# A two-layer image model on one core: the last image's row and column terms through a constant selection tile, and the spectral taps loaded earlier

## The chip, the cores and the metric

The kernel runs on one core of one Trainium2 chip. The metric is the time of one execution on the device in microseconds (us). Three runs of the kernel before gave 9375.59, 9384.07 and 9384.95, so the median is 9384.07 us. Everything is float32.

The profile speaks of five engines: PE (TensorE, matrix multiplies; its weight loads are listed apart as PEld), DVE (VectorE), ACT (ScalarE), POOL (GpSimd) and SP (SyncE, which here does nothing but issue DMA transfers, in the order of its queue). A fp32 matrix multiply shows as two or more PE instructions, a transpose as one. PEclk is the TensorE clock that was granted, 1.00 being full speed.

## The reference

The input `x` is four images of 64 x 64 tokens with 128 channels. Two layers follow, each with a convolution-like part and a feed-forward part; all normalizations (`ln`) are per token over the 128 channels.

```python
# layer 0
x = x + ss2d(ln(x))                 # four selective scans per image, 256 channels, 16 states
t = x as [B, 4096, 128]
p = softmax(ln(t) @ gate_w.T + gate_b, over the 4096 tokens)   # 64 experts
v, idx = top_k(p per expert, 8)                  # each expert picks 8 tokens
pooled = sum_k v[k] * ln(t)[idx[k]]              # [64 experts, 128]
o = gelu(pooled @ w1 + b1) @ w2 + b2             # 128 -> 512 -> 128, per expert
t[idx[k]] += v[k] * o                            # scattered back
# layer 1, on the image as [row m, column k, channel]
n = ln(x)
x = x + n @ Wself.T + (sum_k n) @ Wm.T + (sum_m n) @ Wk.T
t = x as tokens; u = ln(t)
t = t + stu(u)        # one of four segment lengths per a one-hot weight
```

Here `(sum_k n) @ Wm.T` is one 128-vector per row of the image, shared by its 64 columns (the row term), and `(sum_m n) @ Wk.T` is one per column, shared by its 64 rows (the column term). `stu` is the sum of a spectral part (a causal convolution over 4096 tokens with 16 long filters, each followed by a 128 x 128 matrix) and an autoregressive part (`ar`: the token and the two before it, times three 128 x 128 matrices).

## The kernel before, in words

The kernel works through the images in sequence. For each image, sixteen-state scans run in chunks; that is the bulk of the span (`hh`, `db`, `da`, `y` in the profile's groups), and while one image is scanned, the earlier image's experts and layer one (`layer1`), and the front of the next one, are worked off in pieces beside it (`beside`). The last image has nothing to run beside, so what follows its scans is a tail of its own:

- `after_scans` makes the last image's gate logits, transposed: `pT`, 64 experts by 4096 tokens, in a pool named `last`.
- `last_experts` (from L1542). `match_replace` makes `rest`, the probabilities with the top eight of each expert struck out (L1617), and the difference `pT - rest` leaves only the picked ones in `pT`. In `turn_back` (L1632) 64 x 128 blocks of `pT` are turned to token-major by matrix multiplies with `turned`, a diagonal matrix of `1/ssum` (one over the softmax sum per expert), eight blocks to a bank `pk_ps`. `pool` (L1640) then gathers: 32 multiplies accumulate into `po_ps`. Then come 64 weight-streamed expert multiplies (`h1_ps`, `h2_ps`, shown as `h_ps`; L1665, L1697), with `w_t` tiles in a ring of 26 buffers refilled by SP; the bias (L1678), the gelu, the transposes, and at last `outE`, the 64 x 128 outputs of the experts, times `1/ssum`.
- `last_layer1` (from L1728). It has two phases, each a loop `for k in range(10)` over eight groups of 512 tokens (eight image rows), staggered so that group `k` is begun while `k-1` and `k-2` are finished. **Phase one**, per group: four multiplies `sc_ps` of `pT` blocks by `outE` (the scatter, L1786), added to `x2` (L1813); normalization; four transposes `xn_ps` (L1773); `sum_blocks` (`rs_ps`, L1367), four multiplies with a constant that yield the 64 column sums and the 8 row sums of the group, copied to `rs_l`; then the bank `z_ps`: per 128-token block (two image rows) one multiply by `wself_t` (L1792) and two 64-row ones, `row_total` broadcast over 64 columns by `wm_t` (L1801), accumulated in the same bank. `add_total` sums the column totals over the groups on GpSimd into `mk`. VectorE adds `z_ps` to `x2` (L1821). Between the phases one multiply by `wk_t` (L1825) makes the column terms, `cols`, a 128 x 128 tile that is the same for every 128-token block. **Phase two**, per group: `cols` added to `x2` (L1851), normalization, store to `u_d` (L1849), transposes `u_ps`, ScalarE's copy `uT_l`, twelve multiplies `ar_ps` (L1839), the weighted add (L1860) and the store to `x3_d` (L1863).
- `spectrum` (from L1893). It opens with the loads of `taps` (four DMAs, 128 x 4096, L1903) and of the first two `vt` tiles (four each, L1923), then issues the loads `zs` of the normalized tokens (`u_d`, L2041). `taps_of` multiplies `vt` with `taps` into `sp_ps` (L1914), evicted to `wt` (L1918); between its steps the last image's tokens are transformed (`slots_of`). The rest of the spectrum's blocks follow, then `endings`.

What sets the order: the program is written once and a scheduler in the framework orders each engine's instructions by dependence and readiness, with tile pools limiting how many buffers are alive. A tile that is taken from a pool waits for the buffers that held its place before; a pool that opens where another closed waits for the latter's readers. Inside `last_layer1`, `pin(begin)` fixes the order of TensorE, ScalarE, VectorE and GpSimd as written. SP's queue of DMA issues is not pinned. `bank` takes the next of eight one-bank PSUM tiles. `kr` is the pool `last` (right side of the on-chip memory), which is closed before `spectrum` opens its own pools `sp_t` and `sp_w` on the same side.

Of the kernel before, what the change touches and what calls it, by code (L numbers as in the profile page):

```python
# [110 lines left out]
def kernel(  # L111
# [1433 lines left out]
    def last_experts(b, last, pieces):  # L1545
# [5 lines left out]
        with tc.tile_pool(name="tl", bufs=1) as tl:  # L1551
# [62 lines left out]
            turned = tl.tile([E, E], F32, name="turned_a")  # L1614
            with tc.tile_pool(name="tr", bufs=2) as tr:
# [4 lines left out]
                nc.vector.tensor_scalar(turned, ident[0:E, 0:E], ssum, None, ALU.mult)  # L1620
# [7 lines left out]
                def turn_back(g):  # L1628
                    ps = bank([P, 8, E], "pk_ps")
                    for q in range(8):  # L1630
                        t0 = (8 * g + q) * P
                        nc.tensor.matmul(  # L1632
                            ps[:, q, :], pT[:, t0 : t0 + P], turned, start=True, stop=True
                        )
# [39 lines left out]
            with tc.tile_pool(name="tm", bufs=1) as tm:  # L1674
# [3 lines left out]
                nc.vector.tensor_add(h1, hps, b1t)  # L1678
# [46 lines left out]
        last_layer1(b, pT, outE, x2)  # L1725
        xr.__exit__(None, None, None)

    def last_layer1(b, pT, outE, x2):  # L1728

        with tc.tile_pool(name="ll", bufs=2) as lp:  # L1730
            rs = lp.tile([P, 8, W + 8], F32, name="rs_l", bufs=1)
            mk = lp.tile([P, 2, W], F32, name="mk_l", bufs=1)
            begin = len(traced)
# [41 lines left out]
            for k in range(10):  # L1775
                g = k - 2
                if g >= 0:
# [3 lines left out]
                    add_total(mk, rs, g)  # L1781
                if k < 8:
# [6 lines left out]
                if g >= 0:  # L1789
                    z = ps[g, "z"] = four("z_ps")  # L1790
                    for q in range(4):
# [4 lines left out]
                            start=(q == 0),  # L1796
                            stop=False,
                            skip_group_check=True,
                        )
                        for i in range(2):  # L1800
                            nc.tensor.matmul(  # L1801
                                z[i * W : (i + 1) * W, q, :],
                                row_total(rs, 8 * g + 2 * q + i),
                                wm_t,
                                start=False,
                                stop=(q == 3),
                                skip_group_check=True,
                            )
# [739 lines left out]
```

## Time and profile before

| quantity | value |
|---|---|
| median of 3 runs | 9384.07 us (9375.59 to 9384.95) |
| the profiled execution's own time | 9385.75 us |
| its span | 9383.6 us, 139970 instructions |
| its mean granted TensorE clock | 0.839 |
| PE / DVE / ACT / POOL busy | 78% / 87% / 65% / 68% |

By stages (us from the start of the span; busy time in us):

| stretch | what runs | PE | DVE | ACT | POOL | clock | DMA share |
|---|---|---|---|---|---|---|---|
| 0 to 7650 | fronts, scans, earlier images | 5794.58 | 7337.50 | 5260.52 | 6313.30 | 0.82 | 0.64 |
| 7650 to 7706 | last image: softmax, match | 23.11 | 9.58 | 26.62 | 12.38 | 0.67 | 0.92 |
| 7706 to 7735 | `turn_back`, `pool` | 28.49 | 6.66 | 2.45 | 3.00 | 0.50 | 0.06 |
| 7735 to 7798 | expert multiplies | 57.64 | 2.60 | 3.03 | 1.80 | 0.93 | 0.95 |
| 7798 to 7880 | layer one, phase one | 78.54 | 25.58 | 22.79 | 2.49 | 0.52 | 0.00 |
| 7880 to 7921 | layer one, phase two | 30.79 | 26.29 | 21.79 | 1.29 | 0.87 | 0.33 |
| 7921 to 7935 | spectral loads | 0.00 | 0.44 | 0.00 | 0.00 | 0.63 | 0.99 |
| 7935 to 7986 | first `taps_of`, last image's tokens | 44.56 | 24.01 | 22.09 | 0.00 | 0.80 | 0.65 |
| 7986 to 9200 | spectrum | 1157.72 | 720.83 | 692.97 | 0.00 | 1.00 | 0.34 |
| 9200 to 9384 | last backward block, endings | 114.95 | 47.91 | 23.28 | 0.00 | 0.83 | 0.79 |

How to read it: busy times of different engines overlap, so a row does not add up to its stretch. Where one engine's busy time fills the stretch, that engine sets the pace. Where none does, the chain of waits tells which wait ended last. The granted clock is a mean over the stretch.

### The profile page before, as it was taken

How to read it: one execution, taken by the hardware profiler on the slowest of the kernel's cores; microseconds unless marked ns; L12 is line 12 of the kernel's file. 1: busy time of each engine (PE TensorE's matmuls, PEld its weight loads, DVE VectorE, ACT ScalarE, POOL GpSimd, SP SyncE). 2: the span in 40 equal slices, each digit the busy share in tenths (PEclk: the TensorE clock that was granted, in tenths of full speed). 3: DMA queues.
4: the chain of work that ended last, by engine and by line, in shares of the span. 5: the costliest groups of instructions: out<-in, count | busy, mean ns of one | idle time of the engine just before them, and what ended most of it. 6: DMA issues, size and time to landing. Idle time of an engine off the chain costs nothing.

```text
span 9383.6 us, 139970 instructions
## 1 busy us (share of the span) xinstructions
PE 7330.4 (78%) x45310; PEld 4733.8 (50%) x45310; DVE 8201.4 (87%) x9342; ACT 6075.5 (65%) x11458; POOL 6334.3 (68%) x5822
## 2 busy tenths in 40 slices
PE   7778787677777777697768777867777668999997
PEld 4445454355444555454544554543555445556663
DVE  8999999989999999999999999999999963566663
ACT  6676777657755576776865676875586752555552
POOL 6778788969888788877978798977888850000000
PEclk8888797668778888798878887878887877999998
DMA  5656657658566656657757657847757764333336
GB/s 168 214 192 209 208 191 246 204 181 251 184 206 224 215 173 207 199 187 244 248 179 246 211 184 226 252 167 237 243 174 216 212 208 142 95 95 95 95 94 182
DMA packets 918577, 1806.24 MB, mean 192 GB/s; under 512 B 86592, under 2 KB 476512, under 8 KB 914136
## 3 DMA queue, kind: packets, MB, share of 16 engines
q1 hardware_dynamic: 917848, 1797.30, 59.8%
q8 instruction: 363, 5.95, 0.3%
q14 instruction: 366, 3.00, 0.1%
HBM read 1554.75 MB, written 242.22 MB: 192 GB/s over the span
## 4 chain that ended last, share of the span: by engine, by line
POOL 33%; PE 23%; issue 15%; DVE 11%; DMA 9%; ACT 8%; SPq 1%; POOLq 0%; DVEq 0%; ACTq 0%
POOL hh L2407 25%; PE sp_ps L1914 10%; DVE hh L2394 5%; PE y L2434 4%; DVE wt L1918 3%; DMA bc<-bc_d 2%; DVE db L2388 2%; ACT da L2334 2%; PE dl_ps L2254 2%; POOL hst L2406 2%; POOL dx L2257 1%; POOL ex L2248 1%; DMA yk<-y_d 1%; PE dt_ps L2229 1%; ACT no_sq L362 1%
## 5 line engine op out<-in xcount | busy, mean ns | idle before, releaser
L2407 POOL TENSOR_TENSOR hh<-hh,bc 128x1024 f32<-128x1024 f32 x2048 | 4829.5, 2359 | 331.0 <-DVE hh L2394 179.1
L2394 DVE TENSOR_TENSOR_SCAN hh<-da,hst,db 128x512 f32<-128x512 f32 x3584 | 4387.0, 1266 | 115.0 <-PE y L2434 64.3
L2434 PE MATMUL y<-ident,hh 128*128 128x128 f32 x16384 | 2622.9, 314 | 1100.1 <-POOL hh L2407 1007.2
L2334 ACT ACTIVATE da<-dl,aneg 128x512 f32<-128x512 f32 x4096 | 2775.7, 717 | 1066.9 <-DVE hh L2394 1053.4
L2434 PEld LDWEIGHTS y<-ident,hh 128*128 128x128 f32 x16384 | 2194.5, 162 | 1986.5 <-POOL hh L2407 1339.2
L2388 DVE TENSOR_TENSOR db<-du,bc 128x512 f32<-128x512 f32 x4096 | 2619.8, 684 | 154.5 <-ACT du L2314 111.6
L2406 POOL COPY hst<-hh 128x2 f32<-128x2 f32 x1792 | 336.5, 188 | 699.8 <-DVE hh L2394 618.0
L1918 DVE COPY wt<-sp_ps 128x1024 f32<-128x1024 f32 x512 | 607.3, 1221 | 183.4 <-PE sp_ps L1914 161.5
L1914 PE MATMUL sp_ps<-vt,taps 32*128 32x256 f32 x8192 | 593.2, 401 | 67.4 <-DVE wt L1918 32.6
L2394 DVE TENSOR_TENSOR_SCAN hh<-da,db 128x512 f32<-128x512 f32 x512 | 595.9, 1203 | 19.9 <-ACT no_r L366 9.6
L1918 ACT COPY wt<-sp_ps 128x1024 f32<-128x1024 f32 x512 | 514.9, 1015 | 136.8 <-PE sp_ps L1914 118.4
L1914 PEld LDWEIGHTS sp_ps<-vt,taps 32*128 32x128 f32 x8192 | 396.3, 186 | 260.2 <-DVE wt L1918 190.3
L1918 DVE COPY zs<-sp_ps 128x1024 f32<-128x1024 f32 x132 | 161.7, 1225 | 363.8 <-DMA gq<-dft_out 132.7
L1914 PE MATMUL sp_ps<-wt,ut 128*32 128x256 f32 x8192 | 450.3, 380 | 2.0 <-ACT ut L1918 2.0
L740 PE MATMUL cv_ps<-xh,diag 128*128 128x512 f32 x864 | 398.6, 597 | 4.6 <-ACT sg_v L409 3.2
L2254 PE MATMUL dl_ps<-ex,ident 128*128 128x512 f32 x508 | 308.9, 697 | 116.5 <-POOL ex L2248 111.4
L2229 PE MATMUL dt_ps<-dts,dtw 8*128 8x512 f32 x508 | 350.8, 796 | 56.6 <-ACT sg_v L409 25.9
L2257 POOL TENSOR_TENSOR dx<-dl,xc 128x1024 f32<-128x1024 f32 x127 | 300.2, 2364 | 98.0 <-ACT dl L2255 91.3
L1914 PEld LDWEIGHTS sp_ps<-wt,ut 128*32 128x32 f32 x8192 | 264.0, 110 | 196.7 <-issue 25.3
L2255 ACT COPY dl<-dl_ps 128x512 f32<-128x512 f32 x254 | 147.0, 579 | 330.0 <-PE dl_ps L2254 328.9
L1918 ACT COPY zs<-sp_ps 128x1024 f32<-128x1024 f32 x132 | 133.6, 1012 | 330.0 <-DMA zf<-zs 212.9
L2248 POOL TENSOR_TENSOR ex<-ex,dx 128x1024 f32<-128x1024 f32 x127 | 299.9, 2361 | 49.3 <-ACT dx L2245 38.4
(391 smaller groups left out, 9127.5 us busy)
## 6 DMA issues: line engine op xcount, KB each, us to landing
bc<-bc_d SPq DMA_DIRECT2D x2048, 512.0 KB
xc<-xc_d SPq DMA_DIRECT2D x128, 512.0 KB
y_d<-ys SPq DMA_DIRECT2D x128, 512.0 KB
w1t<-in_w_dram SPq DMA_DIRECT2D x96, 512.0 KB
w2t<-in_w_dram SPq DMA_DIRECT2D x192, 256.0 KB
yk<-y_d SPq DMA_DIRECT2D x128, 256.0 KB
yk<-y_d SPq DMA_DIRECT2D x256, 128.0 KB
zf<-zs SPq DMA_DIRECT2D x512, 64.0 KB
```

What stands on the lines that cost most here:

```text
L740: nc.tensor.matmul(ps, diag[:, h, t, :], xh[:, 8 * g + dy : 8 * g + dy + 8, dx : dx + W], start=(t == 0), stop=(t == 8),)
L1914: tc.keep_in_program_order(nc.tensor.matmul(*args, **kw))
L1918: tc.keep_in_program_order(copy(dst, src))
L2229: nc.tensor.matmul(ps, dtw[:, k, h * P : (h + 1) * P], dts, start=True, stop=True)
L2254: nc.tensor.matmul(ps, ident, t[:, h], start=t is dl, stop=t is w)
L2257: nc.gpsimd.tensor_mul(dx, dl, xc)
L2334: i_act = nc.scalar.activation(das[t][:, h, :], sizes[t // N][0][:, h, :], AF.Exp, scale=aneg[:, tk, h, t % N : t % N + 1],)
L2388: nc.vector.tensor_mul(db[h], dus[i][h], bcs[s][:, 0, :])
L2394: i_dve = nc.vector.tensor_tensor_scan(o, d0, d1, init, ALU.mult, ALU.add)
L2406: nc.gpsimd.tensor_copy(hsts[t // N][:, :, t % N], hhs[t][:, :, last])
L2407: i_pool = nc.gpsimd.tensor_mul(hhs[t], hhs[t], bcs.pop(t)[:, 1:2, :].to_broadcast([P, 2, SC]))
L2434: i_pe = nc.tensor.matmul(ys[c][:, q, h, :], hhs[t][:, h, q * P : (q + 1) * P], ident, is_transpose=True, start=(n == 0 and k > 0 and q % ...
```

## The change

It has four parts.

1. `turn_back` uses plain transposes; `turned` is gone. The factor `1/ssum` is applied later, to the first expert layer's sum: a constant `rows` (built on GpSimd) spreads `ssum` over the 128 partitions of `h1_ps` by one multiply, and the bias add becomes `h * by_row + b1`.
2. In phase one the `wm_t` multiplies are gone from `z_ps`; the row sums of each group are copied on GpSimd into `rt_l`. After the loop, one bank gets the column terms in partitions 0 to 63 (`mk` by `wk_t`) and the row terms in 64 to 127 (`rt_l` by `wm_t`), which ScalarE copies to `both_l`.
3. A constant tile `place_l`, 128 x 64 x 64, is built by two GpSimd copies: its upper half selects a token's column, its lower half its row. In phase two, `placed(k)` makes the sum of both terms for the four 128-token blocks of a group by four multiplies of `place_l` slices by `both_l`; the add takes that bank in place of `cols`.
4. `pT` becomes the lower 64 partitions of `wide`, a 128 x 4096 tile. `taps` is a view of the same `wide`. Its four loads, and those of two `vt` tiles (which now live in the pool `last`), are written between the phases, and `kr` closes after `spectrum`.

```diff
+            rows = tl.tile([E, P], F32, name="rows_a")
+            nc.gpsimd.memset(rows, 0.0)
+            nc.gpsimd.tensor_copy(
+                rows.rearrange("p (g c) -> p g c", g=G)[:, :, 0:ER],
+                ident[0:E, 0:E].rearrange("p (r g) -> p g r", g=G),
+            )
...
-                nc.vector.tensor_scalar(turned, ident[0:E, 0:E], ssum, None, ALU.mult)
...
-                        nc.tensor.matmul(
-                            ps[:, q, :], pT[:, t0 : t0 + P], turned, start=True, stop=True
-                        )
+                        nc.tensor.transpose(ps[:, q, :], pT[:, t0 : t0 + P], ident[0:E, 0:E])
...
+            by_row = tl.tile([P, 1], F32, name="by_row")
+            ps = bank([P, 1], "row_ps")
+            nc.tensor.matmul(ps, rows, ssum, start=True, stop=True)
+            nc.vector.tensor_copy(by_row, ps)
...
-                nc.vector.tensor_add(h1, hps, b1t)
+                nc.vector.scalar_tensor_tensor(h1, hps, by_row, b1t, ALU.mult, ALU.add)
...
+            both = lp.tile([P, C], F32, name="both_l", bufs=1)
+            place = lp.tile([P, H, W], F32, name="place_l", bufs=1)
+            rt = lp.tile([P, 8, 8], F32, name="rt_l", bufs=1)
+            half = ident[0:W, 0:W]
+            nc.gpsimd.tensor_copy(place[0:W], half.unsqueeze(1).to_broadcast([W, H, W]))
+            half = ident[W:P, W:P]
+            nc.gpsimd.tensor_copy(place[W:P], half.unsqueeze(2).to_broadcast([H, H, W]))
+            vt = last["vt"] = {}
+
+            def load_v(i):
+                vt[i] = last["pool"].tile([P, FB, 2 * BP], F32, name="vt", bufs=2)
+                for g in range(4):
+                    nc.sync.dma_start(vt[i][g * KK : (g + 1) * KK], vd[:, FB * i : FB * (i + 1)])
...
+                    nc.gpsimd.tensor_copy(rt[:, g], rs[:, g, W:])
...
-                            start=(q == 0),
-                            stop=False,
-                            skip_group_check=True,
+                            start=True,
+                            stop=True,
                         )
-                        for i in range(2):
-                            nc.tensor.matmul(
-                                z[i * W : (i + 1) * W, q, :],
-                                row_total(rs, 8 * g + 2 * q + i),
-                                wm_t,
...
-            nc.gpsimd.tensor_copy(mk[:, 1, :], mk[:, 0, :])
-            cols = bank([P, C], "cs_ps")
-            nc.tensor.matmul(cols, mk.rearrange("p i w -> p (i w)"), wk_t, start=True, stop=True)
+            for g in range(4):
+                nc.sync.dma_start(
+                    last["taps"][g * KK : (g + 1) * KK],
+                    md.rearrange("k (j g i) d -> k j g i d", g=4, i=2)[:, :, g],
+                )
+            for i in range(2):
+                load_v(i)
+            z = bank([P, C], "cs_ps")
+            nc.tensor.matmul(z[0:W], mk[:, 0, :], wk_t, start=True, stop=True)
+            nc.tensor.matmul(
+                z[W:P], rt.rearrange("p g j -> p (g j)"), wm_t, start=True, stop=True
+            )
+            nc.scalar.copy(both, z)
+
+            def placed(k):
+                ps[k, "c"] = four("cs_ps")
+                for q in range(4):
+                    r0 = 8 * k + 2 * q
+                    nc.tensor.matmul(
+                        ps[k, "c"][:, q, :],
+                        place[:, r0 : r0 + 2, :].rearrange("p i w -> p (i w)"),
+                        both,
+                        start=True,
+                        stop=True,
+                    )
+
+            placed(0)
             for k in range(10):
                 g = k - 2
+                if k + 1 < 8:
+                    placed(k + 1)
...
-                    nc.vector.tensor_add(
-                        x4(k), x4(k), cols.unsqueeze(1).to_broadcast([P, 4, C])
-                    )
+                    nc.vector.tensor_add(x4(k), x4(k), ps[k, "c"])
...
+                        wide = kp.tile([P, L], F32, name="pT_a")
...
-                            "pT": kp.tile([E, L], F32, name="pT_a"),
+                            "pool": kp,
+                            "pT": wide[0:E],
+                            "taps": wide.rearrange("k (j i d) -> k j i d", i=2, d=C),
...
+    side.pop("pool").close()
+    spectrum(fin["taps"], fin["load_v"], fin["vt"])
     kr.__exit__(None, None, None)
-    side.pop("pool").close()
-    spectrum()
```

More of the change, by code (lines that the diff above doesn't have):

```diff
@@ L1613, in last_experts @@
             pooled = tl.tile([P, E], F32, name="pooled_a")
-            turned = tl.tile([E, E], F32, name="turned_a")
             with tc.tile_pool(name="tr", bufs=2) as tr:
@@ L1724, in last_experts, with last_layer1 @@
             ring.__exit__(None, None, None)
-        last_layer1(b, pT, outE, x2)
+        last_layer1(b, pT, outE, x2, last)
         xr.__exit__(None, None, None)
-    def last_layer1(b, pT, outE, x2):
+    def last_layer1(b, pT, outE, x2, last):
         with tc.tile_pool(name="ll", bufs=2) as lp:
@@ L1732, in last_layer1 @@
             mk = lp.tile([P, 2, W], F32, name="mk_l", bufs=1)
+            both = lp.tile([P, C], F32, name="both_l", bufs=1)
[10 more added lines that the diff above has]
+                    nc.sync.dma_start(vt[i][g * KK : (g + 1) * KK], vd[:, FB * i : FB * (i + 1)])
+            last["load_v"] = load_v
             begin = len(traced)
@@ L1795, in last_layer1 @@
                             wself_t,
-                            start=(q == 0),
-                            stop=False,
-                            skip_group_check=True,
-                        )
-                        for i in range(2):
-                            nc.tensor.matmul(
-                                z[i * W : (i + 1) * W, q, :],
-                                row_total(rs, 8 * g + 2 * q + i),
-                                wm_t,
-                                start=False,
-                                stop=(q == 3),
-                                skip_group_check=True,
-                            )
+                            start=True,
+                            stop=True,
+                        )
                 if 0 < k < 9:
@@ L1850, in last_layer1 @@
                 if k < 8:
-                    nc.vector.tensor_add(
-                        x4(k), x4(k), cols.unsqueeze(1).to_broadcast([P, 4, C])
-                    )
+                    nc.vector.tensor_add(x4(k), x4(k), ps[k, "c"])
                     moments(k)
@@ L1892, in to_slots, with spectrum @@
             yield from pipelined(BP // 8, (0.5, load), None, (2.0, turn), None, (1.0, put))
-    def spectrum():
+    def spectrum(taps, load_v, vt):
         with ExitStack() as pools, tc.tile_pool(
@@ L1900, in spectrum @@
         ) as spw, tc.tile_pool(name="sp_ps", bufs=4, space=PSUM) as sps:
-            taps = spt.tile([P, C // 8, 2, C], F32, name="taps", bufs=1)
-            for g in range(4):
-                nc.sync.dma_start(
-                    taps[g * KK : (g + 1) * KK],
-                    md.rearrange("k (j g i) d -> k j g i d", g=4, i=2)[:, :, g],
-                )
             wt = spw.tile([P, C // 4, FB * 2 * BP, 4], F32, name="wt")
-            u1, fq, vt, ut, zq, gq = {}, {}, {}, {}, {}, {}
+            u1, fq, ut, zq, gq = {}, {}, {}, {}, {}
             def banks():
@@ L1918, in out @@
                 tc.keep_in_program_order(copy(dst, src))
-            def load_v(i):
-                vt[i] = spt.tile([P, FB, 2 * BP], F32, name="vt")
-                for g in range(4):
-                    nc.sync.dma_start(vt[i][g * KK : (g + 1) * KK], vd[:, FB * i : FB * (i + 1)])
             def load_u(i):
@@ L2034, in spectrum @@
             n = NQ // FB
-            load_v(0)
-            load_v(1)
             ub = {}
```

## The prediction

> **What bounds the kernel now.** I read the page first (share of the span by engine, then the slices), then the busy time of the tail in stretches of 5 us with the granted clock, then the chain of work that ended last from 7600 us on, and last the SP queue around 7920 us. The page:
>
> ```profile
> span 9383.6 us, 139970 instructions
> ...
> PE   7778787677777777697768777867777668999997
> ...
> DVE  8999999989999999999999999999999963566663
> ...
> PEclk8888797668778888798878887878887877999998
> ```
>
> Up to 7650 us VectorE sets the pace (9 tenths in nearly every slice); the change hardly touches that part. The edits lie in the tail, 7650 to 7990 us, where little overlaps. Two stretches there (columns: PE, weight load, DVE, ACT, POOL busy with counts, granted clock, DMA share, GB/s), the first in phase one of layer one, the second in phase two:
>
> ```profile
> 7810.00:7815.00 5.00, 5.00 (x24) 3.31 (x23) 1.43 (x9) 0.50 (x2) 0.00 (x0) 0.50 0.01 3
> ...
> 7895.00:7900.00 5.00, 4.27 (x39) 4.03 (x38) 3.51 (x20) 3.42 (x10) 0.18 (x1) 1.00 0.36 108
> ```
>
> Phase one is bound by TensorE at half clock: 5.00 of 5.00 busy, clock 0.50, all others under a third. Phase two runs at clock 1.00. The chain that ended last (start, duration, engine, tile, line, instructions):
>
> ```profile
> 7701.01 4.49 DVE rest_a L1617 x2
> ...
> 7706.46 7.06 PE pk_ps L1632 x32
> 7713.52 3.60 PE po_ps L1640 x16
> 7717.13 3.60 PE pk_ps L1632 x16
> ...
> 7743.43 9.43 DMA w_t<-in_w_dram
> ...
> 7814.16 1.05 PE xn_ps L1773 x4
> 7815.21 1.61 PE rs_ps L1367 x8
> 7816.83 2.00 PE sc_ps L1786 x8
> ...
> 7901.18 2.94 PE ar_ps L1839 x24
> ...
> 7920.69 0.76 DVE x_a L1860
> 7922.60 0.63 SPq L1903
> 7924.61 10.50 DMA vt<-vd
> 7935.25 2.22 PE sp_ps L1914 x13
> ```
>
> Phase one is TensorE and nothing else, in a period of 10.07 us (xn_ps at 7814.16 and again at 7824.24). Between 7921.45 and 7935.25 every engine waits for the spectral loads. SP's queue there:
>
> ```profile
> 7917.28 4.55 SPq L1863 DMA_DIRECT2D x_d<-x_a  x2
> 7921.92 2.65 SPq L1903 DMA_DIRECT2D taps<-md  x4
> 7924.61 10.59 SPq L1923 DMA_DIRECT2D vt<-vd  x8
> 7935.25 2.67 SPq L2041 DMA_DIRECT2D zs<-u_d  x4
> ```
>
> **1. Transposes for scaled matmuls (L1632).** Each `turned` matmul is two instructions, a transpose is one. In the chain 16 pk_ps take 3.60 us, 0.225 each; a transpose in phase one takes 1.05/4 = 0.26 and is wider. I take 0.225, so a group of eight falls from 3.60 to 1.80 us. The last two groups gain 1.8 each. The first two (7.06 us) gain less: VectorE subtracts until 7711.35 and only then empties the first bank (0.69), so the first pooling matmul starts at 7712.1, not 7713.52: 1.4. `turned` itself leaves VectorE ahead of the match (0.25 and a gap: 0.35). Sum 5.0 + 0.35 = **-5.3**. Bounds: -2 (0.45 a transpose, only the start gained) and -7. The shift carries through the weights: their loads stood still at a DMA share of 0.00 to 0.02 from 7710 to 7735 for want of free buffers, which the expert matmuls free.
>
> `rows` on GpSimd, its matmul with `ssum`, the 128x1 copy and the scaled bias add: GpSimd is idle there from 7662 to 7669, TensorE waits 0.36 us for the mask, and the add is 0.75 for 0.69. **0**; without that cover 0.8.
>
> **2. Row terms out of phase one (L1801).** Per iteration the z block takes 10.07 - 1.05 - 1.61 - 2.00 = 5.41 us: eight wself instructions and sixteen narrow wm ones, in turns of 0.73 and 0.63. What stays is eight wself instructions in one run. Counted as in the mix they are 0.365 each (2.92, a gain of 2.5); but the first ar_ps block has the same shape in one run, 24 in 4.49 us, half clock until about 7890.6 and 0.123 each after: 0.23 each at half clock, so 1.9. This is the nearest row, and I take a gain of 3.5, times 8: **-28**; bounds -20 and -29. What is late next: the chain bank, ACT copy of rs_l (0.22), four normalizations (1.65), transposes is 3.6 us and a VectorE round 3.9 (0.69 + 1.23 + 0.69 + five of 0.2), both under the new 6.5 us period. So TensorE still bounds it, if the clock stays at 0.50.
>
> Does it stay? In the 75 us before, a z block of 5.4 us without a gap did not open the gate; after, the longest run of full-width matmuls is 1.9 us. I say it stays shut. If it opens, VectorE's 3.9 to 4.5 bounds the period and another 10 to 16 us go.
>
> [...] The trace shows 0.50 through 75 us of a fully busy TensorE, so the measurement decides.
>
> GpSimd gets two copies into `place` (64x4096) once the last w_t load has landed (about 7795), and eight 128x8 copies. Nearest rows: a memset of 128x2048 in 1.80 and a product of 128x512 in 1.27, so 3.6 to 10 us each, done by 7815 at the latest; the first reader comes some 35 us later. **0**; uncovered up to 20.
>
> **3. Between the phases.** Before, the wk matmul (0.8) ran under VectorE's last z add and x_a of phase two was ready 1.5 us after the last z matmul. After: two half-width matmuls (four instructions, 0.9), ACT copy of 128x128 (0.3), four selection matmuls (1.8), VectorE 0.7, with 0.1 for each hand-over: 3.9. **+2.4**; bounds +1.5 (clock open) and +3.
>
> **4. Phase two.** Its period is 4.11: ar_ps 2.95, u_ps 0.60, and about 0.7 in which TensorE waits for ACT's uT copy. Four selection matmuls are eight instructions of 0.123, 0.98, and are queued just where TensorE waits: 0.3 to 0.45 beyond the wait, in five iterations (the other three blocks run ahead): +2.2. Against it, they run 5 us without a gap before the first ar block, which was at half clock (4.49 for 2.95): 0 to -1.5, I take -0.7. Sum **+1.5**; bounds 0 and, if the gate closes, (1.05 + 1.9 + 5.6) - 4.11 = 4.4 in seven iterations, +31.
>
> **5. Spectral loads.** The built order on SP is not quite "between the phases": two of the four loads of `taps`, to partitions 64 to 127 where no probabilities lie, and the first eight of `vt` stand far ahead, in the last scans (about 7133 and the 150 us after); only two stand between the phases, behind the last sc_ps. Those two have some 19 us until SP's first u_d store (2 MB took 10.6 us before, so 5.3). The wait of 7921.45 to 7935.25 goes: **-13.7**. Late next: SP's loads of zs, issued 0.4 us after the end of phase two instead of at the first matmul, the second one behind the landing of the last x3 store (about 3 us); the first consumer came 6.1 us after the first spectral matmul, so both are in time. Bounds: -8 if that chain stalls, -18 if the cold stretch of 7959 to 7975 (fu matmuls 3.78 for 1.98) also goes.
>
> Among the scans, a load of 512 KB (2.65 us by the same rate) now stands on SP ahead of ub<-u_d, and there the chain runs x_d store, ub load (4.75), TensorE: **+1**; bounds -3 (a pair of TensorE's matmuls moves too) and +6. The bc loads behind it are issued five steps of 3.53 us ahead.
>
> **Sum.** -5.3 - 28 + 2.4 + 1.5 - 13.7 + 1 = -42.1. The profiled execution took 9385.75 (span 9383.6 and 2.15 around it), so 9343.6; the median of the runs, 9384.07, is 1.7 lower: **9342**.
>
> **The rivals.**
> (a) The gate opens in phase one. For it: a denser z block. Against: its run is shorter than those that did not open it. -42 - 14: 9328.
> (b) The gains are small: wself keeps 0.365 (-20), the zs chain stalls (-8), pk_ps gains 2: 9384 - 20 - 8 - 2 + 5 = 9359.
> (c) Phase two falls to half clock for the selection matmuls: -42 + 31 - 2: 9371. Against it: it gets denser, not thinner.
> (d) Slower: SP holds at the hoisted taps load, which waits for an ACT eviction of the earlier element's layer one, and bc loads stand behind it. Five steps are 17.7 us; only a hold beyond 17.7 + 42 = 60 us makes the kernel slower; at 80 us it gives 9404. Against it: SP's next entries, the x_d stores, waited for the later GpSimd add of the same pieces anyway.
> (e) The change does nothing for the spectrum, because zs is the real wait: 9342 + 13.7 = 9356.
>
> **How the numbers follow.** Forecast 0.57 (own range 9333 to 9350), (a) 0.20, (b) and (e) 0.12, (c) 0.06, (d) 0.05. Two tenths are left out below 9320 and above 9360. About 0.2%, 19 us, is what a measurement can tell from no change: 9365 to 9403 is "the same". Faster: forecast, (a), (b), (e), 0.89; same: (c), 0.06; slower 0.05.
>
> **What the changed profile would show.** Phase one: xn_ps to xn_ps in 6.5 us at clock 0.50, eight wself in 1.9, no z_ps of 64 columns. pk_ps eight in 1.8. Phase two: 4.5 us at 1.00, no wait of ar_ps for uT. The first sp_ps within 1 us of the last x_a, with no DMA in the chain between. The forecast is wrong if phase one's clock differs from 0.50 (below 9335), if phase two's is under 0.9 (above 9360), or if the stretch before 7650 changes by more than 6 us.

## The result, and the profile after

The changed kernel takes 9322.92 us (median of four runs, 9317.88 to 9329.90), the kernel before 9382.28 in the runs beside it (9375.59 to 9384.95). The ratio is 0.9941, with a 95% interval of 0.9930 to 0.9953, so it is 59 us faster. The forecast was 9342, with a range of 9320 to 9360. The time lies inside it, near its lower end.

The profiled execution took 9321.34 us with a span of 9319.6. These are the rows of its page that answer to those shown of before:

```profile
span 9319.6 us, 139792 instructions
...
PE   7778787577777777787868777768777768999996
...
DVE  8999999989999999999999999999999974556663
...
PEclk8889797668778888798878897868888878999998
```

In the first 32 slices no digit differs by more than one from before. What differs lies in the slices of the tail, and the chain that ended last shows how (start, duration, engine, tile, line, instructions):

```profile
7694.91 4.49 DVE rest_a L1622 x2
7699.43 5.84 DVE pT_a L1628 x6
7705.26 0.61 DVE pk_a L293
7705.92 3.68 PE po_ps L1642 x16
7709.60 1.04 PE pk_ps L1636 x8
7710.64 3.60 PE po_ps L1642 x16
...
7793.04 3.46 DVE a_l L1779
...
7800.91 2.00 PE sc_ps L1808 x8
7802.91 2.00 PE z_ps L1814 x8
7804.92 0.85 PE xn_ps L1794 x4
7805.77 1.08 PE rs_ps L1367 x8
7806.85 1.10 PE sc_ps L1808 x8
7807.97 0.70 DVE x_a L1825
...
7868.56 2.96 PE ar_ps L1877 x24
7871.62 0.76 DVE x_a L1896
7872.42 1.16 PE sp_ps L1944 x16
```

Three things are to be seen. The eight `z_ps` instructions run in one piece of 2.00 us, and right after them `xn_ps`, `rs_ps` and `sc_ps` take about half of what they took (1.10 for 2.00): the granted clock has gone from 0.50 to 1.00, at 7806.14 (the gate has opened, as it is called here), and the chain now goes over VectorE and ScalarE as well as TensorE. A VectorE product of 128x4 elements takes 3.46 us. And the first spectral multiply starts 0.04 us after the last `x_a`, with no transfer between.

The clock by stretches of 5 us (PE, weight load, DVE, ACT, POOL busy with counts, granted clock, DMA share, GB/s), in phase one:

```profile
7805.00:7810.00 5.00, 5.00 (x39) 4.80 (x38) 3.37 (x16) 2.83 (x9) 0.45 (x2) 0.89 0.00 0
...
7815.00:7820.00 5.00, 5.00 (x42) 4.59 (x40) 4.24 (x18) 3.57 (x11) 0.70 (x4) 1.00 0.00 0
```

Before, the same phase stood at 0.50 from end to end (the clock was 0.50 from 7801.88 to 7890.63).

From the starts of the instructions on each engine, the tail falls into stages. All times are us; a stage runs from the start of the work named first to the start of the work named second, or to its end where the table says so. "Predicted" is the term on record for it. The 2.49 us from `spread` to the first `sc_ps` are the same in both and are left out.

| stage | before | after | change | predicted |
|---|---|---|---|---|
| match (`rest_a`) to first `h_ps` | 34.31 | 27.84 | -6.47 | -5.3 |
| first `h_ps` to the last copy of the experts (`spread`) | 60.37 | 63.81 | +3.44 | 0 |
| first `sc_ps` to first `xn_ps` | 5.33 | 8.62 | +3.29 | 0 |
| first `xn_ps` to the end of the last `z_ps` | 76.76 | 32.83 | -43.93 | -28 |
| end of the last `z_ps` to first `ar_ps` | 7.08 | 9.10 | +2.02 | +2.4 |
| first `ar_ps` to the end of the last `x_a` | 34.09 | 32.77 | -1.32 | +1.5 |
| end of the last `x_a` to first `sp_ps` | 13.81 | 0.05 | -13.76 | -13.7 |
| first `sp_ps` to the first multiply with `ut` | 50.91 | 49.21 | -1.70 | 0 |

The column of changes adds up to -58.4. The profiled execution is 64.4 us shorter than that of before; of the other 6, 6.1 lie ahead of the match, which started at 7694.91 instead of 7701.01. That is a difference of executions: one and the same kernel, `grouped` below, ran twice with a profile and had its match at 7682.22 and at 7700.42. The matches of all thirteen profiles lie between 7682.22 and 7702.16, without a pattern by edit. So the time of a kernel as a whole spreads by some 20 us, and the stages of the tail are the better measure. Where nothing was changed most of them agree to a fraction of a microsecond (phase one took 76.76 in three kernels); the experts' stage spreads by 1.7 us (60.04 to 61.76 in six profiles that leave it as it was) and the last stage by 3.2 (49.01 to 52.20), so the -1.70 in the last row can't be told from nothing. The stages carry the verdicts below.

### The profile page after: what moved, and what is told of

It is laid out like the page before. It is cut to its first block, busy times and chain, and to the rows that moved or that the text cites. A ratio compares the mean times of both kernels' runs of the same rounds, so it can differ in the third digit from the quotient of the medians.

```text
span 9319.6 us, 139792 instructions
## 1 busy us (share of the span) xinstructions
PE 7286.4 (78%) x45218; PEld 4705.1 (50%) x45218; DVE 8204.7 (88%) x9342; ACT 6078.9 (65%) x11459; POOL 6345.1 (68%) x5833
## 4 chain that ended last, share of the span: by engine, by line
POOL 34%; PE 24%; issue 15%; DVE 10%; ACT 8%; DMA 7%; SPq 1%; POOLq 0%; DVEq 0%; ACTq 0%
POOL hh L2433 26%; PE sp_ps L1944 10%; DVE hh L2420 5%; PE y L2460 4%; DVE wt L1948 3%; ACT da L2357 3%; DVE db L2414 2%; PE dl_ps L2277 2%; POOL hst L2432 2%; DMA bc<-bc_d 2%; POOL dx L2280 2%; POOL ex L2271 1%; DMA yk<-y_d 1%; ACT no_sq L362 1%; PE cv_ps L740 1%
## 5 line engine op out<-in xcount | busy, mean ns | idle before, releaser
L1944 PE MATMUL sp_ps<-vt,pT_a 32*128 32x256 f32 x8192 | 592.6, 400 | 53.1 <-DVE wt L1948 32.8
L1944 PEld LDWEIGHTS sp_ps<-vt,pT_a 32*128 32x128 f32 x8192 | 394.7, 185 | 246.9 <-DVE wt L1948 190.4
```

The costliest lines, as they stand in the source:

```text
L1944: tc.keep_in_program_order(nc.tensor.matmul(*args, **kw))
```

## The experiments

### Each part alone

**The transposes.** The kernel before with the first part of the change only:

```diff
-                        nc.tensor.matmul(
-                            ps[:, q, :], pT[:, t0 : t0 + P], turned, start=True, stop=True
-                        )
+                        nc.tensor.transpose(ps[:, q, :], pT[:, t0 : t0 + P], ident[0:E, 0:E])
...
+            by_row = tl.tile([P, 1], F32, name="by_row")
...
-                nc.vector.tensor_add(h1, hps, b1t)
+                nc.vector.scalar_tensor_tensor(h1, hps, by_row, b1t, ALU.mult, ALU.add)
```

> Only the transposes of the picked probabilities are changed (with the factor 1/ssum moved to the first expert layer). In the changed kernel the stretch from the match to the first expert multiply was 27.9 us against 34.3 before, a gain of 6.4, but at the end of the experts only 3.0 of it were left, and the weight loads ran at 387 GB/s instead of 406. Theory one: the weights are the limit of the experts, and most of an earlier start is lost again: the stretch is 27.9, the gain at the end of the experts 3, the total -3. Theory two: the slower weight loads were a difference of executions: the gain of 6 holds to the end, total -6. The row terms, the spectral loads and the time up to 7650 us are as before.

Measured: match to first `h_ps` 27.83 us, then 63.23 to the last copy of the experts instead of 60.37. From the match to the first `sp_ps` it is 231.19 against 234.24, so -3.05. In the time as a whole that can't be seen: 9378.34 against 9382.76, ratio 0.9998 (0.9989 to 1.0008). The first theory gave the right amount. But its reason is incomplete: the weight loads were slower here too, at 382 to 386 GB/s, while the three kernels without this part that were profiled beside it (`rows_only`, `loads_only` and `wide_terms`) reached 406 to 408 at best. Why is taken up below (`aligned`).

**The row and column terms.** The kernel before with the second and third part:

```diff
-                        for i in range(2):
-                            nc.tensor.matmul(
-                                z[i * W : (i + 1) * W, q, :],
-                                row_total(rs, 8 * g + 2 * q + i),
-                                wm_t,
...
-                    nc.vector.tensor_add(
-                        x4(k), x4(k), cols.unsqueeze(1).to_broadcast([P, 4, C])
-                    )
+                    nc.vector.tensor_add(x4(k), x4(k), ps[k, "c"])
```

> Only the row and column terms are changed (constant tile, selection multiplies in phase two); the transposes and the spectral loads are as before. Theory one: without the narrow multiplies the clock gate opens in phase one, whatever stands around it: granted clock 1.00 from the second group on, phase one from the first transpose to the last z_ps about 33 us against 76.8, a stall of 3.3 us in VectorE's 128x4 product while GpSimd builds the constant tile, 13.8 us of spectral loads still to wait for, total about -39. Rival: the gate opened by the chance of where its window fell; then the clock stays at 0.50, the period of a group is about 7 us, phase one about 53 us, total -20.

Measured: phase one 33.01 us, the first `xn_ps` 8.80 after the first `sc_ps` (5.33 before), phase two 32.87, 13.94 of wait for the loads. The time is 9340.22 against 9382.76, ratio 0.9957 (0.9942 to 0.9972), so -42.5. Phase one takes what it takes in the changed kernel, where the clock went to 1.00 (32.83), and not the 76.76 of the kernel before, at 0.50: the gate opened in another program too, and it was not the chance of one execution.

**The spectral loads.** The kernel before with the fourth part:

```diff
+                        wide = kp.tile([P, L], F32, name="pT_a")
...
+                            "taps": wide.rearrange("k (j i d) -> k j i d", i=2, d=C),
...
-    spectrum()
+    spectrum(fin["taps"], fin["load_v"], fin["vt"])
```

> Only the place and time of the loads of the taps and the first two vt tiles are changed. The wait of 13.8 us between phase two and the first spectral multiply goes; total -13.8 if nothing else moves. The changed kernel was also 6.1 us earlier at the match (7694.9 against 7701.0), long before any of its edits. Theory one: that comes of the two loads of taps and the eight of vt that stand far ahead among the scans; then it is here too, and in neither of the kernels without these loads: total -20. Theory two: it is a difference of executions: total -14, and the match starts at 7701 or anywhere within 6 us of it in all of them.

Measured: last `x_a` to first `sp_ps` 0.06 us instead of 13.81. The match starts at 7699.84 against 7701.01, with the same loads standing among the scans, so theory two holds: these loads cost and gain nothing that can be told from the spread. The time is 9369.42 against 9382.76, ratio 0.9986 (0.9976 to 0.9995): -13.3.

From the match to the first `sp_ps`, the three parts give -3.05, -39.70 and -11.47 alone, which makes -54.2; together they gave -56.7. `loads_only` lost 1.4 us in the experts, which lies within that stage's spread, and 0.9 in phase two, which the full change did not.

### What shuts the gate in phase one

**The same row terms at full width.** The row totals are spread by GpSimd into a 128x512 tile, so that one multiply with 128 columns of weights takes the place of two with 64:

```diff
-                        for i in range(2):
-                            nc.tensor.matmul(
-                                z[i * W : (i + 1) * W, q, :],
-                                row_total(rs, 8 * g + 2 * q + i),
+                        nc.tensor.matmul(
+                            z[:, q, :],
+                            rw[:, q * P : (q + 1) * P],
```

> The kernel before with one change in phase one: the row totals are spread by GpSimd to a 128x512 tile per group, and each 128-token block adds its row terms by one multiply of full width (128 columns of weights) instead of two of 64. The same sums, in as many streamed columns. Theory one: the gate counts how much of the time columns stream through the whole array, and narrow multiplies that wait for their weights do not count; then it opens here in the first or second group, although the row terms are still there: period under 6 us, clock 1.00, phase one 35 to 45 us against 76.8, total -30 to -40. Rival: what shut the gate is the accumulation of row terms as such, or opening it needed the work to be gone; then the clock stays 0.50, the z block is 16 instructions of 0.25, the period 8.7 us, total about -11.

Measured: phase one 38.65 us, period 4.35, and the clock in its second and third stretch is

```profile
7810.00:7815.00 5.00, 5.00 (x31) 4.93 (x32) 3.22 (x15) 1.30 (x4) 0.00 (x0) 0.69 0.02 3
7815.00:7820.00 5.00, 5.00 (x44) 4.78 (x42) 3.30 (x16) 3.51 (x10) 1.43 (x3) 1.00 0.00 0
```

The row terms are still there and the gate is open, from the second of these stretches on. It is not the work that had to go. The time was 9349.01 in its one run, against 9382.76.

**The same multiplies in another order.** The kernel before with one line more, a second loop over the blocks, so that the four wself multiplies of a group stand ahead of its eight narrow ones:

```diff
                             wself_t,
                             start=(q == 0),
                             stop=False,
                             skip_group_check=True,
                         )
+                    for q in range(4):
                         for i in range(2):
```

> The kernel before with the same multiplies in another order: in each group's z block the four wself multiplies come first, then the eight narrow ones, instead of one and two in turns. After sc_ps there are then 4.0 us of wide multiplies in a row (2.00 of sc_ps, eight z_ps instructions of 0.25), as many as stood before the opening in the kernel with the row terms taken out. Theory one: the gate asks for a few us in which columns stream nearly all the time, wherever narrow ones stand after; it opens in one of the first groups, and phase one takes 45 to 60 us instead of 76.8. Rival: narrow multiplies in every group keep the mean share too low; clock 0.50 throughout, and phase one only gains what the turns cost: per group 2.0 + 2.5 instead of 5.4 us, phase one about 70 us.

Measured: 38.70 us for phase one, and 9325.88 in its one run (its match came 18.8 us early). TensorE's instructions there (start, duration, line, operation, tiles, shape):

```profile
7785.40 1.63 PE L1773 MATMUL xn_ps<-ident,xn_l 128*128 128x128 f32 x4 [3.28 <-ACT xn_l L383]
7786.82 1.82 PE L1367 MATMUL rs_ps<-totals,xn_l 128*128 128x72 f32 x8
7788.57 2.07 PE L1786 MATMUL sc_ps<-outE_a,pT_a 64*128 64x128 f32 x8
7790.58 2.07 PE L1792 MATMUL z_ps<-wself_t,xT_l 128*128 128x128 f32 x8
7792.58 1.48 PE L1802 MATMUL z_ps<-wm_t,rs_l 128*64 128x128 f32 x16
7793.99 0.66 PE L1773 MATMUL xn_ps<-ident,xn_l 128*128 128x128 f32 x4
7794.49 1.01 PE L1367 MATMUL rs_ps<-totals,xn_l 128*128 128x72 f32 x8
```

The first group alone opens the gate: 4.0 us in which `sc_ps` and `z_ps` instructions of 128 streamed columns follow each other at 0.25 us, and before the narrow ones are through everything runs at about twice the speed (granted clock 0.66 in the stretch 7790 to 7795, 1.00 in the next). This is the whole change: no instruction was removed, and 38 of the 44 us of phase one are gained. The same kernel, timed in four runs:

> The same kernel as grouped (the kernel before, with the four wself multiplies of a group ahead of its eight narrow ones and nothing else), timed. Its profile had phase one at 38.7 us against 76.8 and all other stages of the tail as before; so -38, about 9343, if the opening of the gate comes in every execution. Rival: it depends on where the run of wide multiplies falls, and comes only in some executions; then the runs spread between 9343 and 9380.

Measured: 9341.94 (9337.25 to 9350.23, four runs) against 9381.58, ratio 0.9957 (0.9941 to 0.9972), so -40; phase one 38.89 in its profile. All four times lie below the lowest one of the kernel before (9367.96), so the gain came in each of the four.

**Narrow work behind an open gate.** The changed kernel, with the narrow multiplies put back from the fourth group on as extra work whose result the next multiply overwrites:

```diff
+                        for i in range(2 if g >= 3 else 0):
+                            nc.tensor.matmul(
+                                z[i * W : (i + 1) * W, q, :],
+                                row_total(rs, 8 * g + 2 * q + i),
+                                wm_t,
+                                start=True,
+                                stop=True,
+                            )
```

> The changed kernel, with the narrow multiplies of the row terms put back as extra work from the fourth group on (g of 3 to 7): each block's two narrow ones go into the z bank just ahead of the wself multiply that overwrites them. The first three groups open the gate as in the changed kernel. Theory one: a narrow stretch counts as idle, so the open gate shuts again within one or two groups, the groups with narrow work go back to a period of 10 us, and phase one is 33 + 5 x 5 = about 60 us. Rival: the gate only has to be opened once and narrow work keeps it open: then the period at full clock is half of 10.07, 5.0 us, against 3.8 now, and phase one is about 39 us.

Measured: phase one 41.85 us; two stretches in its narrow part:

```profile
7820.00:7825.00 5.00, 5.00 (x42) 3.76 (x41) 2.92 (x15) 2.96 (x8) 0.45 (x2) 1.00 0.00 0
7825.00:7830.00 5.00, 5.00 (x44) 3.93 (x42) 3.25 (x15) 2.96 (x8) 0.45 (x2) 1.00 0.22 63
```

The rival holds: wide and narrow multiplies in turns, which stood at 0.50 for 77 us in the kernel before, kept the clock at 1.00 here, once it was open, with a period of 5.5 us. The time was 9331.90 in its one run. So in this run the gate opened behind 4.0 us of wide multiplies (`sc_ps` and `z_ps`, 7801.60 to 7805.68; the clock is 0.76 in the stretch 7805 to 7810 and 1.00 in the next) and stayed open through multiplies in turns that had not opened it in the kernel before.

How much opening takes is not settled. In eight profiles the wide multiplies of phase one stand together and the clock is still at 0.50 when it begins. In seven of them it opened before, or within 2 us after, the first group's wself multiplies were through: 1.2 us after in the changed kernel (7806.14 against 7804.92), about 0.8 in `grouped` and 1.7 in `narrow_late` by the mean clock of the stretch; for `rows_only` its phase one of 33.01 us alone speaks for it. In the eighth, `aligned` of the next section, it opened only behind the second group's:

```profile
7800.26 2.07 PE L1808 MATMUL sc_ps<-outE_a,pT_a 64*128 64x128 f32 x8
7802.26 2.07 PE L1814 MATMUL z_ps<-wself_t,xT_l 128*128 128x128 f32 x8
...
7806.73 2.07 PE L1808 MATMUL sc_ps<-outE_a,pT_a 64*128 64x128 f32 x8
7808.73 2.07 PE L1814 MATMUL z_ps<-wself_t,xT_l 128*128 128x128 f32 x8
7810.60 0.95 PE L1794 MATMUL xn_ps<-ident,xn_l 128*128 128x128 f32 x4
```

The first group's 4.0 us run is the same as in the changed kernel, but the instructions behind it kept their times at half clock (`rs_ps` 1.82 us at 7804.98, `sc_ps` and `z_ps` 2.07), and only the `rs_ps` at 7811.38 took 1.01. In the profiles of the kernel before and of the changed kernel the clock stands at 0.50 or 1.00 for whole multiples of 3.41 us (but for the two ends of the record): in the latter it goes to 1.00 at 7806.14, to 0.50 at 7836.86 and to 1.00 at 7840.27, which is nine of them and one. Whether it matters where a run falls between two such marks is not shown, nor whether `sc_ps`, with 64 rows of weights (`64*128` in the lines) where the others have 128, counts for less. In the three profiles of the old order (the kernel before, `pk_only`, `loads_only`) phase one took 76.76 us; in the first of them the clock was 0.50 through the whole of it.

### The slower weight loads

```diff
-            by_row = tl.tile([P, 1], F32, name="by_row")
+            by_row = tl.tile([P, 64], F32, name="by_row")[:, 0:1]
```

> The changed kernel with a 128x64 tile for by_row, of which one column is used, instead of 128x1. In both kernels with by_row the w_t buffers lie 32 bytes off a multiple of 256 in their partitions, in the four without it on a multiple of 256; the weight loads run at 384 to 387 GB/s in the former and at 400 to 408 in the latter. Theory one: the start of the buffers sets the rate. Then the loads run at 406 GB/s here, the time from the first expert multiply to the second layer's last copy falls from 63.8 to about 60.4 us as in the kernel before, and the kernel gains 3 us in its profile. Rival: the rate goes with something else in these programs; 387 GB/s and 63.8 us stay.

Measured, in the stretch 7770 to 7775 of the changed kernel and then of this one (the last column is GB/s):

```profile
7770.00:7775.00 5.00, 5.00 (x16) 1.08 (x16) 0.00 (x0) 0.00 (x0) 0.00 (x0) 1.00 1.05 387
```

```profile
7770.00:7775.00 5.00, 5.00 (x17) 1.10 (x16) 0.00 (x0) 0.00 (x0) 0.00 (x0) 1.00 1.05 406
```

Theory one holds. In the built programs the first `w_t` buffer starts at byte 73472 of its partition in the kernel before, at 73760 in the changed one (288 x 256 + 32) and at 73984 (289 x 256) here. The experts take 60.59 us instead of 63.81, with nothing changed but 252 unused bytes per partition and the start of the buffers behind them. The experts' stage takes 63.23 to 63.81 us in the four profiles with `w_t` off a multiple of 256 (`after`, `pk_only`, `narrow_late`, `tuned`) and 60.04 to 61.76 in the other nine. The kernel as a whole took 9322.68 in its one run; its match was 2.65 us later, and phase one took 34.76, because the gate opened a group later, so the 3.2 us can't be seen there.

### Further edits to the changed kernel

Three edits to the changed kernel. The tile `place` moves into the storage of `tt`, which is free after the pooling; the loads of the tokens' later slices are issued once their half of the buffer has been read; `by_row` is 64 bytes wide.

```diff
+            place = tt.rearrange("p n (i w) -> p (n i) w", w=W)
...
-                ub[g] = spt.tile([P, BP // 8, 2, C], F32, name="zs", bufs=4)
+                if g < 4:
+                    ub[g] = spt.tile([P, BP // 8, 2, C], F32, name="zs", bufs=4)
+                else:
+                    ub[g] = ub[g - 4]
...
+                if g + 4 < BP // 8:
+                    load_s(g + 4)
                 uo = ub[g][:, :, 1, :]
```

> The changed kernel with three changes. The constant tile place is written into the storage of tt as soon as the pooling has read it, while VectorE has nothing to do, so that VectorE's product of two small tiles need not wait for GpSimd: the time from the first sc_ps to the first xn_ps falls from 8.6 to 5.3 us. by_row is 64 bytes wide, which puts the w_t buffers on a multiple of 64, though not of 256: 63.8 to 60.4 us for the experts if 64 is enough, 63.8 if not. The loads of the last four slices of normalized tokens go to the same buffers' first half as soon as the multiplies have read it, not after the store of the transformed slice has landed: the first taps_of takes 41 to 46 us instead of 49.2. Together -6 to -14 against the changed kernel's 9322.9: 9309 to 9317. If the store was not what the loads waited for, the last part gains nothing.

Measured: 9316.69 (9303.97 to 9321.38) against 9378.39, ratio 0.9930 (0.9916 to 0.9944). That interval overlaps the changed kernel's (0.9930 to 0.9953), so the times alone don't tell the two apart; by stages, from the match to the first multiply with `ut` it takes 217.56 us against 226.72. First `sc_ps` to first `xn_ps` is 5.33 us again. GpSimd and VectorE in the changed kernel, where the stall was (GpSimd first, then VectorE):

```profile
7789.20 3.59 POOL L1743 COPY place_l<-ident 64x4096 f32<-64x4096 f32 x1 [64.88 <-DVE outE_a L1728]
7792.85 3.62 POOL L1745 COPY place_l<-ident 64x4096 f32<-64x4096 f32 x1
```

```profile
7792.84 0.16 DVE L1778 SCALAR_TENSOR_TENSOR a_l<-mv_l,r_l 128x4 f32<-128x4 f32 x1 [0.73 <-ACT r_l L1771]
7793.04 3.45 DVE L1779 TENSOR_TENSOR a_l<-a_l,r_l 128x4 f32<-128x4 f32 x1
7796.52 0.17 DVE L1780 TENSOR_SCALAR a_l<-a_l 128x4 f32<-128x4 f32 x1
```

The product `a_l` times `r_l` ends with GpSimd's second copy (7792.85 + 3.62 = 7796.47); in `tuned`, where the copies run at 7722 and 7726, the same product takes 0.16. The experts took 63.47 us at 387 GB/s, so 64 bytes are not enough and 256 are. The first `taps_of` took 43.52 instead of 49.21: the loads had waited for the store.

Then extra multiplies whose results nobody reads were added ahead of the pooling and ahead of phase one, with `by_row` at 256 bytes:

```diff
+                warm = bank([P, 4, C], "warm_ps")
+                for _ in range(5):
+                    nc.tensor.matmul(warm, tt[:, 0, :], tt[:, 0:4, :], start=True, stop=True)
...
+                if k == 1:
+                    warm = four("warm_ps")
+                    for _ in range(3):
+                        nc.tensor.matmul(warm, wself_t, place[:, 0:8, :], start=True, stop=True)
```

> The version with place built early and the tokens' loads early, with by_row 256 bytes wide, so that w_t lies on a multiple of 256, and with extra multiplies whose results nobody reads: five of 128x512 from tt while VectorE makes the match, and three of 128x512 between the second sc_ps and the first xn_ps. If narrow work keeps an open gate open but cannot open it, the pooling (pk_ps and po_ps, 27.8 us with the match, clock 0.50 so far) now runs at 1.00: its 16.5 us of TensorE after the subtraction fall towards 9, the stretch from the match to the first expert multiply to 19 to 22 us. The first group of phase one, 7 us at half clock, runs at full clock: 32.9 falls to 29 to 30. The experts take 60.4 us instead of 63.5. In all -12 to -15 against the version without these (its profile 9308.7). Rival: the pooling is bound by something besides the clock, or the gate shuts on narrow work in the cold stretch; then 27.8 stays or grows by the extra multiplies, at most 2 us, and the phase gains only its 3 us.

Measured: 9310.51 (9305.58 to 9314.89) against 9381.58, ratio 0.9925 (0.9913 to 0.9938). The second group of extra multiplies did what was expected: phase one 29.27 us instead of 32.94, and the experts, with `by_row` at 256 bytes, took 60.19. The first did not: match to first `h_ps` 27.83, as without. From the match to the first `sp_ps` it is 167.14 us against 174.04 in `tuned`, so -6.9 of the -12 to -15 expected. TensorE idles between their end and the pooling (4.19 us ahead of the first transposes), and the clock is 0.50 again in the stretch from 7705. So twelve instead of five:

> As warm, with twelve extra multiplies of 128x512 in place of five ahead of the pooling. The five ran from 7692.4 to 7698.8 and the clock was 1.00 there, but TensorE then stood idle for most of 7699 to 7708 and the gate was shut again when the pooling began. Twelve end about 7706.5, just as the pooling can begin. Theory one: the open gate is kept by the pooling's narrow transposes and multiplies: clock 1.00, the stretch from the match to the first expert multiply falls from 27.8 to 19 to 21 us, and the experts, whose weights start to flow earlier by the same time, keep their 60 us: -7 to -9 against warm. Rival: the pooling multiplies load 128 columns of weights for 64 streamed ones, so the gate sees them as idle and shuts again within a window or two: 24 to 28 us, no gain in the time.

Measured: the stretch is 26.82 us, the time 9308.09 (9306.46 to 9311.19), ratio 0.9927 (0.9914 to 0.9941): no gain over `warm` that can be told. The first pooling multiplies, and the clock around them:

```profile
7709.23 0.96 PE L1640 MATMUL pk_ps<-ident,pT_a 64*128 64x64 f32 x12
7710.77 0.46 PE L1640 MATMUL pk_ps<-ident,pT_a 64*128 64x64 f32 x4 [0.58 <-DVE pT_a L1632]
7713.17 2.66 PE L1646 MATMUL po_ps<-pk_a,tt_a 128*128 128x64 f32 x16 [1.94 <-DVE pk_a L293]
7715.76 1.11 PE L1640 MATMUL pk_ps<-ident,pT_a 64*128 64x64 f32 x8
7716.81 3.67 PE L1646 MATMUL po_ps<-pk_a,tt_a 128*128 128x64 f32 x16
```

The gate is open when the pooling begins (twelve transposes in 0.96) and shut about 1 us into the first `po_ps` run: the granted clock is 0.93 in the stretch 7710 to 7715 and 0.50 in the next, where sixteen take 3.67 as before. Whether the pooling's own density shuts it, 64 streamed columns for 128 loaded ones, or the 0.58 and 1.94 us of waiting just ahead, these runs don't tell. The extra multiplies ahead of phase one ran at half clock (5.21 us for 2.84 in `warm`), because the clock had fallen (0.78 in the stretch 7790 to 7795, 0.53 in the next), so the first `xn_ps` came 7.96 us after the first `sc_ps` instead of 5.33. They opened the gate all the same (clock 1.00 in the stretch from 7800): phase one then took 28.40 us.

## Why the prediction came out as it did

The sign, the place and the range were right, and of the single terms the spectral loads (-13.7, measured -13.76) and the step between the phases (+2.4, measured +2.02). But the likeliest case did not happen: it had the gate shut. By the prediction's own sign, a clock other than 0.50 in phase one with a time below 9335, its forecast was wrong. That the time still lies in the range is in part luck: two costs that were put at nothing, 3.44 and 3.29 us, offset part of what the gate gave beyond the forecast. Without them the time would have been about 9316, an estimate (9322.92 - 6.73), outside the range.

- **Row terms, -28, measured -43.9.** The mechanism (TensorE bounds phase one, and less of it is left) held for the first group only. The step that failed is "I say it stays shut". It rested on two readings. One, "a z block of 5.4 us without a gap did not open the gate", took a busy TensorE for a dense one; `grouped` shows the same instructions opening it in another order. The other, "the longest run of full-width matmuls is 1.9 us", overlooked that `sc_ps` with its 2.00 us of the same instruction rate stands directly ahead: 4.0 us (how much of `sc_ps` counts is not shown, see `aligned`). This was rival (a), which had a chance of 0.20 and 10 to 16 us more; phase one gave 15.9 more. Its reason, a denser z block, agrees with `grouped`, where the order alone was changed.
- **What bounds phase one then.** "VectorE's 3.9 to 4.5 bounds the period": the period after the opening is 3.78 us (`sc_ps` at 7806.85, 7814.40 and 7821.96, two groups apart), just under that range. VectorE is busy for 4.24 of 5 us, but it is not the bound by itself: the chain that ended last goes from TensorE (`sc_ps` 1.10) over VectorE (from `x_a` at 7807.97 to 7811.50) and ScalarE (`xn_l` 1.66) back to TensorE, once in two groups.
- **"0.50 through 75 us of a fully busy TensorE, so the measurement decides".** The measurement was of one order of the multiplies, and the busy time of the profile does not tell orders apart. In `grouped` TensorE was busy for 5.00 of 5 us in the stretch 7790 to 7795, as in the kernel before in 7805 to 7810, and the clock opened after a dense run of 4.0 us; in the old order the longest such run was 2.7 us (`sc_ps` 2.00 and two `z_ps` 0.73). The same 4.0 us did not open it in the first group of `aligned`, so the length of the run alone does not decide.
- **GpSimd's copies into `place`, 0, measured +3.3.** The step asked only when `place` is first read, not whom the copies disturb. VectorE stood for 3.45 us in the product of `a_l` and `r_l`, until the second copy ended; in `tuned`, without a copy beside it, the product takes 0.16. Not every VectorE instruction was held: the add of `sc_ps`, during the first copy, took 0.69 (0.69 in `tuned`). What tells the two apart is not shown.
- **Transposes, -5.3, measured -6.5 and then +3.4.** A transpose of 64x64 takes 0.13 us (1.04 for eight), not 0.225, so this stage gained more than was said. "The shift carries through the weights" was wrong by more than half of it. The cost lies in `by_row`, which was put at 0: `aligned` gives back 3.2 of the 3.4 us. Its 128x1 tile moved the start of the weights' buffers from a multiple of 256 bytes to 32 bytes past one, and the loads slowed from 406 to 387 GB/s.
- **Phase two, +1.5, measured -1.3.** The gate was open for nearly all of its first `ar_ps` block (clock 1.00 from 7840.27, the block from 7839.80: 2.96 for 4.49), which gives all of the 1.5 us of which half was counted. The +2.2 for the selection multiplies did not come: at 0.89 a block they fit into the time that TensorE had waited for ScalarE (0.73 us in the last blocks, which have no selection multiplies beside them), and the period stayed at 4.11 (`cs_ps` at 7847.26 and 7851.37).
- **Spectral loads.** As worked out, down to the loads of `zs` being in time. **Scans, +1:** nothing that can be told from the spread of executions.

## What to carry to other kernels

A busy TensorE at a granted clock of 0.50 can be an order problem before it is a work problem: put the wide multiplies of a group next to each other (4.0 us of them here) and see whether the clock opens; here that alone gave 40 us without removing an instruction. A helper tile of a few bytes moves every buffer behind it, so look at the transfer rate after adding one (387 GB/s instead of 406 here), and try its size rounded to 256 bytes, which gave the 406 back. And a large GpSimd copy belongs where VectorE is idle, not merely where its result is not yet needed: here a product of 0.16 us took 3.45 beside one.

## What the runs showed of the hardware that was not expected

- The same work ran at either clock. Wide and narrow multiplies in turns (0.73 and 0.63 us) stood at 0.50 for 77 us in the kernel before, where the gate was shut, and at 1.00 in `narrow_late` (0.41 and 0.37 us), where it was open. What the gate weighs is not shown: in the first group of `aligned` columns streamed at the dense rate for 4.0 us, and it stayed shut.
- Opened, phase one takes 32.8 to 34.8 us in the four profiles of kernels that have it as in the changed one (the changed kernel, `rows_only`, `aligned`, `tuned`). In the changed kernel, `aligned` and `tuned` the first group starts at half clock (its first `rs_ps` takes 1.82 us, 1.01 later on), and in `aligned`, the slowest, the second group's `sc_ps` and `z_ps` still take 2.07 each (1.16 in the third).
- The start of a buffer within its partition set the rate of its loads in these kernels: at best 387 GB/s at 32 or 64 bytes past a multiple of 256, 406 to 408 at a multiple of 256. From 406 to 387 is a loss of 4.7%. What causes it is not shown.
